# A macaron block with fp4 feed-forward layers on one Trainium2 core: the weights prepared by two ways, a new order of loads and of work, and small scale products moved between engines

## The chip, the cores and the metric

The kernel runs on one core of a Trainium2 chip. A core has five engines that work side by side, each through its own queue of instructions in the order in which they were issued: TensorE (PE in the profile, with its weight loads as PEld), VectorE (DVE), ScalarE (ACT), GpSimd (POOL), and SyncE (SP), which here issues all DMA transfers. Engines wait for one another by semaphores. Operands lie in SBUF (128 partitions), the sums of TensorE in PSUM (eight banks of 512 f32 values per partition). The metric is the time of one execution on the device in microseconds (us); lower is better.

## The reference

The input x has 4 sequences of 2048 rows of 256 values, f32. Three sublayers are added to it in turn:

```python
x = x + 0.5 * ffn(layernorm(x), w_gate, w_up, w_down)
x = x + attention(layernorm(x), Wq, Wk, Wv)      # one head, causal, scale 1/16
x = x + 0.5 * ffn(layernorm(x), w_gate, w_up, w_down)

def fp4_quant_dequant(x):                        # blocks of 16 along the last dim
    scale = maximum(max(abs(xb)) / 6, 1e-12)     # one scale a block
    idx = searchsorted(_MID, abs(xb / scale))    # nearest of 0, .5, 1, 1.5, 2, 3, 4, 6
    return _GRID[idx] * sign(xb) * scale

def fp4_linear(x, w):                            # both sides are quantized, then expanded
    return einsum('bsk,nk->bsn', fp4_quant_dequant(x), fp4_quant_dequant(w))

def ffn(x, w_gate, w_up, w_down):                # 256 -> 704 -> 256
    h = silu(fp4_linear(x, w_gate)) * fp4_linear(x, w_up)
    return fp4_linear(h, w_down)
```

Both feed-forward layers use the same three weights. The weights are f32 in memory and are quantized by the kernel itself, at its start. A quantized value is a short fp4 number times an f32 block scale, and the result has to be nearly f32-exact, so the kernel splits such a value into two f16 numbers, a high and a low part, and makes each product from three products of TensorE (high by high, high by low, low by high).

## The kernel before

**Tiles and steps.** The 8192 rows are worked on in 32 tiles of 2 x 128 rows, eight to a sequence. For a tile the stages are: load, layernorm (`layernorm`, line 629), quantization of its rows (`ffn_x`, 695), gate and up products (`ffn_gu`, 717), quantization of the hidden values (`ffn_h`, 740), down products and addition to the rows (`ffn_down`, 773), layernorm, attention (`attn_x`, `attn_vy`, `attn_scores`, `attn_exp`, `attn_pv`), and the feed-forward stages once more. The function `step(n)` (995) records one stage of each of several tiles: the scores of tile n, the first feed-forward layer of tile n + 4, the second one of tile n - 2, the load of tile n + 6. The last tile's second layer is done in two single halves of 128 rows.

**The order.** No operation is issued where the code names it. All calls go to a recorder (`Record`, 153), which notes each operation with what it depends on and a cost (`_cost`, 207). Afterwards `order` (238) plans: it runs the list of operations forwards and backwards through a model of the five engines (`_pass`, 269), with three policies of ten rounds each, and keeps the pass that ends first. A policy says how far ahead of readiness an operation may be taken and how waiting weighs against rank. The model knows of a slower TensorE after an idle window, of DMA bandwidth, and of times in which GpSimd stands while VectorE has certain operations. `rec.emit(rec.order())` (1064) then issues everything in the planned order; that is why every instruction of the profile has the same line, L339, the line of the emitting call. Which instruction is which is read from its operands' names.

**The start.** SyncE issues the loads in planned order: the first tile of x (xt), four parts of the gate and up weights (gu, of eleven blocks of 64 gate and 64 up rows three in each of the first three parts and two in the last), the down weights (dwork), the attention weights and further tiles. `prepare_gu` (510) takes for each part the block maxima (VectorE), reciprocals, divides and rounds (`cut`, 492), finds the largest scale over all parts (mx, one transpose by TensorE, one product with ones), multiplies the rounded numbers by their scaled block scales (`factors`, 502, and `times`, 486) to an f32 tile, and transposes that by f32 products with the identity matrix `ident` into PSUM, 22 blocks of 128 x 128. The high part is a ScalarE copy to f16, the low part a product that takes the high part away (`minus`, minus the identity) and a second copy. `prepare_dn` (570) does the same for the down weights, in 22 more blocks, and `prepare_attn` for the attention weights.

**The main products.** `ffn_gu` has for each of the two row halves j of a tile four groups of products, gate and up, each in two PSUM banks of 352 columns (u):

```python
T.matmul(pu[:, u, :UH], qT[:, 4 * j + 2 * a + c, :], wguT[:, b, c, c0 : c0 + UH],
```

with UH = 352; the moving operand is one run of 352 columns. A group of gate products (pg) is followed by the SiLU on ScalarE, and a group of up products (pu) by a product on VectorE that writes h. There is one buffer of two banks for each, so the next half's gate products wait for the SiLU of the last. SiLU and the softmax's exponential need different tables of ScalarE; a table load is an instruction of its own in ScalarE's queue.

**Block scales of activations.** `ffn_x` and `ffn_h` reduce a tile's blocks to their maxima (sx: xs in the profile for the rows, hs for the hidden values), take the reciprocal, round on ScalarE and VectorE (`round_e2m1`, 669), and multiply the rounded numbers with the high and the low part of the scale (`halves`, 682). The two parts are

```python
S.activation(pairs(sh), twice(sx), AF.Copy, scale=2.0**23)
V.scalar_tensor_tensor(pairs(sl), twice(sx), 2.0**23, pairs(sh), ALU.mult, ALU.subtract)
```

in `ffn_x` (xsh, xsl), and with the tile's own power of two `pt` in place of 2**23 in `ffn_h` (hsh, hsl; hmt, het and hpt are one value per partition). A DMA transpose on SyncE's queue then turns the f16 halves into xqT or hT, the operands that TensorE holds.

**Attention.** `attn_scores` copies the scores from PSUM with running maxima, and ends with nb, one value per row (the maximum times a scale, plus 15 ln 2, on VectorE), the bias of the exponential in `attn_exp`. `attn_pv` ends with rc, the reciprocal of the row's sum, times kv, a constant per partition, and the addition to xt. The names `ps` (scores), `po` (attention outputs, down products) are PSUM pools of two buffers each.

**GpSimd** has, besides constants at the start, seven operations of two columns per layernorm (`ve`, `rs` by a power, `r2` three times, `rs`, `nm`, with a letter ahead: f, a or g for the first, second and third layernorm).

Of the kernel before, what the change touches and what calls it, by code (L numbers as in the profile page):

```python
# [22 lines left out]
P = 128  # L23
# [32 lines left out]
ROUNDS = 10  # L56
POLICIES = ((100.0, 60.0), (150.0, 60.0), (200.0, 60.0))
# [95 lines left out]
class Record:  # L153


    def __init__(self):
        self.ops, self.pools = [], []
# [4 lines left out]
    def add(self, engine, real, method, args, kwargs):  # L162
# [8 lines left out]
        op.index, op.deps, op.after = len(self.ops), {}, []  # L171
# [35 lines left out]
    def _cost(self, op):  # L207
# [6 lines left out]
        if op.engine == "PE":  # L214
            t = (max(n, 64) / 2.4 + 2.2) * (4 if op.ins[0].dtype == F32 else 1)
            return t, t + 65
# [5 lines left out]
        if op.engine == "POOL":  # L222
            t = 110 if op.method == "memset" else 850 if ALU.pow in op.args else 350
            return t, t
# [13 lines left out]
    def order(self):  # L238
# [18 lines left out]
        best = None  # L257
        for policy in POLICIES:
            rank = {op: 88.0 * op.index for op in self.ops}
            for _ in range(ROUNDS):  # L260
                start, out, end = self._pass(rank, False, *policy)
                if best is None or end < best[0]:
                    best = (end, out)

                back, _, _ = self._pass({op: -start[op] - op.busy for op in self.ops}, True, *policy)
                rank = {op: -back[op] - op.busy for op in self.ops}
        return best[1]

    def _pass(self, rank, back, soon, patience):
# [3 lines left out]
        waiting = {e: [] for e in free}  # L273
# [12 lines left out]
        while len(out) < len(self.ops):  # L286
# [8 lines left out]
            t, e = best  # L295
            now = [op for op in waiting[e] if ready[op] <= t + soon]
# [24 lines left out]
            elif e == "POOL" and op.method != "memset":  # L321

                alone = 775.0 if ALU.pow in op.args else 270.0
# [3 lines left out]
            free[e] = t + op.busy + (more if e in ("PE", "POOL") else 0.0)  # L327
            end = max(end, t + op.late + more)
            for u, lag in nxt[op]:
                ready[u] = max(ready[u], t + lag + more)  # L330
# [26 lines left out]
def macaron(ctx: ExitStack, tc: tile.TileContext, x, wqT, wkT, wv, wgu, wdn, out):  # L357
# [19 lines left out]
    wguT = const.tile([P, 2, 2, 2 * DF], F16, name="wguT")  # L377
# [70 lines left out]
    GP.memset(ones, 1.0)  # L448
    minus = const.tile([P, P], F16, name="minus")
    S.activation(minus, ident, AF.Copy, scale=-1.0)  # L450

    def load_gu():
        for r, t in zip(gparts, gus):
            SY.dma_start(t, wgu[:, r, :])

    def load_rest():
        SY.dma_start(dn, wdn.rearrange("(c p) d -> p c d", p=P))
        for t, w in ((qk[:, 0], wqT), (qk[:, 1], wkT), (va[:, 0], wv)):
            SY.dma_start(t, w.rearrange("(c p) d -> p c d", p=P))

    def behind(first, op):
# [3 lines left out]
        return op  # L465

# [638 lines left out]
```

## Time and profile before

| what | value |
|---|---|
| median of three runs | 1200.46 us (1198.76, 1200.46, 1201.81) |
| the profiled execution's own time | 1200.17 us |
| its span (first to last instruction) | 1198.5 us |
| granted TensorE clock, mean | 0.999 of full speed |
| TensorE busy | 1161.6 us, 8723 matrix products |
| of it gate and up products, 352 columns, 3072 | 515.3 us |
| of it down products, 256 columns, 2176 | 264.9 us |
| VectorE, ScalarE, GpSimd busy | 1055.1, 849.4, 245.8 us |

Matrix products overlap one another in the records: a product of 352 columns has a record of 312 ns, but the starts of two neighbours are 149 ns apart. How much TensorE can do is therefore read from the distances of starts, and where it stands idle from the busy time by stages or the instructions in order of time. In such a list each row has the start, the duration, the engine, the line, the operation, output <- inputs by name (by partitions x elements and type), how many neighbours of the same kind are put together in the row, and in square brackets the idle time ahead of it and what ended that. A row of a group of instructions has, after the bar, the busy time of the group, the mean of one in ns, and the idle time before its instructions. The 40 slices of the page are 30 us long each; a digit is the busy share in tenths. The record of a busy TensorE does not show by itself that it works at its peak.

### The profile page before, as it was taken

The page shows a single profiled execution, that of the slowest core. Times are in us where ns is not written, and L with a number is a line of the kernel's source. Part 1 is how long each engine was busy: PE and PEld are TensorE (multiplying, and loading weights), DVE is VectorE, ACT ScalarE, POOL GpSimd, SP SyncE. Part 2 cuts the span into 40 slices and gives each one's busy share as a digit, 9 for nine tenths or more (in the row PEclk, how much of TensorE's full clock was granted, in tenths as well). Part 3 has the DMA queues.
Part 4 walks back from the last instruction along what each step waited for, and adds up shares of the span by engine and source line. Part 5 has one row for each costly group of instructions (what it writes and reads, how often), then busy time and mean ns, then how long its engine had stood idle before and what let it go on. Part 6 is the DMA issues. An engine that isn't in the chain of part 4 may idle for free.

```text
span 1198.5 us, 23996 instructions
## 1 busy us (share of the span) xinstructions
PE 1161.6 (97%) x8723; PEld 851.7 (71%) x8723; DVE 1055.1 (88%) x2674; ACT 849.4 (71%) x1704; POOL 245.8 (21%) x706
## 2 busy tenths in 40 slices
PE   3999999999999999999999999999999999999997
PEld 2677777777687777776777777777768777776675
DVE  7989999998779999998887999999877999978776
ACT  7768987677477987674776887677647876656552
POOL 4023321222022221121212230121202221110020
PEclk9999999999999999999999999999999999999999
DMA  6245555765464555655655556777557556646553
GB/s 213 52 76 102 97 96 114 133 122 103 81 130 92 116 101 116 125 105 103 131 95 94 110 87 111 130 133 115 101 96 113 92 92 105 105 93 105 101 111 84
DMA packets 450087, 128.27 MB, mean 107 GB/s; under 512 B 432048, under 2 KB 449200, under 8 KB 449968
## 3 DMA queue, kind: packets, MB, share of 16 engines
q1 hardware_dynamic: 449968, 126.74, 56.6%
q8 instruction: 68, 1.11, 0.4%
q14 instruction: 51, 0.42, 0.1%
HBM read 11.34 MB, written 8.39 MB: 16 GB/s over the span
## 4 chain that ended last, share of the span: by engine, by line
PE 66%; DVE 14%; ACT 13%; issue 3%; POOL 3%; DMA 1%; SPq 0%; DVEq 0%; ACTq 0%
PE po L339 28%; PE pg L339 15%; PE pu L339 14%; PE ps L339 9%; DVE h L339 4%; ACT xn L339 4%; DVE hs L339 2%; ACT sc L339 2%; ACT L339 2%; ACT h L339 1%; ACT pp L339 1%; DVE sc L339 1%; DVE xt L339 1%; DVE xs L339 1%; ACT hf L339 1%
## 5 line engine op out<-in xcount | busy, mean ns | idle before, releaser
L339 PEld LDWEIGHTS <-xqT 128*128 128x128 f16 x3072 | 299.9, 98 | 158.0 <-issue 7.5
L339 PE MATMUL po<-wdT,hT 128*128 128x256 f16 x2176 | 264.9, 274 | 5.6 <-DVE xt L339 5.2
L339 PE MATMUL pg<-wguT,xqT 128*128 128x352 f16 x1536 | 257.9, 312 | 4.9 <-ACT h L339 3.9
L339 PE MATMUL pu<-wguT,xqT 128*128 128x352 f16 x1536 | 257.4, 312 | 0.0
L339 PEld LDWEIGHTS <-hT 128*128 128x128 f16 x2176 | 213.5, 98 | 43.1 <-DMA hT<-h 4.7
L339 PE MATMUL ps<-xT,y 128*128 128x512 f16 (+2 forms) x960 | 201.2, 347 | 1.5 <-DVE sc L339 1.2
L339 PE MATMUL po<-vv,pT 128*128 128x257 f16 (+1 forms) x1632 | 194.9, 272 | 1.1 <-DMA pT<-pp 1.1
L339 PEld LDWEIGHTS <-pT 128*128 128x128 f16 x1632 | 157.8, 97 | 33.9 <-DMA pT<-pp 2.2
L339 DVE TENSOR_TENSOR h<-h,pu 128x704 f32<-128x704 f32 x128 | 112.9, 882 | 58.7 <-PE pu L339 41.1
L339 ACT ACTIVATE h<-pg,cgu 128x704 f32<-128x704 f32 x128 | 107.9, 843 | 78.9 <-PE pg L339 78.2
L339 PEld LDWEIGHTS <-y 128*128 128x128 f16 x960 | 90.6, 98 | 71.9 <-issue 3.0
L339 ACT ACTIVATE hf<-h 128x1408 f16<-128x1408 bf16 (+1 forms) x65 | 88.0, 1353 | 58.6 <-DVE h L339 58.5
L339 ACT ACT_TABLE_LOAD x90 | 115.5, 1283 | 2.3 <-PEq L1098 0.8
L339 ACT ACTIVATE sc<-sc,nb,ksc 128x128 f32<-128x128 f32 (+7 forms) x64 | 82.8, 1293 | 35.3 <-DVE nb L339 34.8
L339 DVE TENSOR_TENSOR h<-h,hinv 128x1408 f32<-128x1408 f32 (+1 forms) x65 | 103.7, 1595 | 0.5
L339 DVE TENSOR_REDUCE hs<-h 128x88 f32<-128x1408 f32 (+1 forms) x65 | 103.5, 1592 | 0.7
L339 DVE TENSOR_SCALAR_CACHE_REDUCE sc<-ps 128x512 f32<-128x512 f32 (+2 forms) x144 | 84.4, 593 | 11.2 <-PE ps L339 11.1
L339 POOL TENSOR_SCALAR gve<-gsq 128x2 f32<-128x2 f32 (+1 forms) x33 | 8.2, 249 | 415.9 <-ACT xn L339 415.9
L339 DVE TENSOR_TENSOR pp<-sc,pp 128x1024 f16<-128x1024 f32 (+4 forms) x96 | 86.4, 908 | 4.9 <-ACT pp L339 4.5
L339 POOL TENSOR_SCALAR ave<-asq 128x2 f32<-128x2 f32 x32 | 15.7, 492 | 318.4 <-ACT xn L339 213.5
L339 ACT CAST pp<-sc 128x1024 f16<-128x1024 f32 (+4 forms) x96 | 73.0, 787 | 0.4
L339 DVE SCALAR_TENSOR_TENSOR xt<-po,het,xt 128x256 f32<-128x256 f32 x128 | 60.0, 470 | 13.4 <-PE po L339 13.2
(158 smaller groups left out, 1601.0 us busy)
## 6 DMA issues: line engine op xcount, KB each, us to landing
xt<-x SPq DMA_DIRECT2D x32, 256.0 KB, 3.2
out<-xt SPq DMA_DIRECT2D x31, 256.0 KB, 2.6
pT<-pp SPq DMA_TRANSPOSE x152, 3.1
hT<-h SPq DMA_TRANSPOSE x128, 3.8
gu<-wgu SPq DMA_DIRECT2D x3, 384.0 KB, 7.4
xqT<-xn SPq DMA_TRANSPOSE x65, 3.2
xT<-xs SPq DMA_TRANSPOSE x64, 2.5
dwork<-wdn SPq DMA_DIRECT2D x1, 704.0 KB, 7.2
```

The lines of the kernel that those rows point to most:

```text
L339: op.call(*map(real, op.args), **{k: real(v) for k, v in op.kwargs.items()})
```

## The change

The diff has six parts.

- **Loads.** All loads from memory are chained in one order (`fetch`), the gate and up parts 1st, 3rd, 4th and 5th, with the first tile of x 2nd; the second tile is 6th, then the down weights and the attention weights.
- **Weights by two ways.** The first two gate/up parts are still transposed by TensorE, but with `is_transpose`, 12 blocks for the 22, and so are the 22 blocks of the down weights. The last two parts are made as f16 high and low halves directly (VectorE products with a high and a low block scale), and a DMA transpose each, on SyncE's queue, writes them to the weights' tile. The expanded scales (`factors`) go from VectorE to ScalarE.
- **Layout of the weights.** wguT goes from (high/low, k half, 1408 columns) to (11 blocks, high/low, k half, gate/up, 64). The gate and up products become 384 and 320 columns wide (six and five runs of 64 in memory) in place of 352 and 352; in PSUM the 704 results are contiguous across the border of the two banks.
- **Low parts of block scales.** hsl and xsl go from VectorE to GpSimd as plain subtractions. For that sx is scaled beforehand: in `ffn_x` by 2**23 within the operations that are there (undone in the rounding's scale), in `ffn_h` by a new ScalarE product of hs with hpt.
- **Small products of attention.** nb and the product of rc with kv go from VectorE to ScalarE.
- **The planner.** Fifteen policies of six rounds for three of ten; each pass is judged by TensorE's lost time before and after 500 us separately, and the best first half and the best second half are joined through a blended rank. A third term, `lead`, can pull the work of the start (layernorm, quantization of the first tile, and the gate/up weights) ahead. Costs of transposes, of GpSimd and of its waits are changed.

The diff, cut to its core:

```diff
--- before.py
+++ after.py
...
-ROUNDS = 10
-POLICIES = ((100.0, 60.0), (150.0, 60.0), (200.0, 60.0))
+ROUNDS = 6
+POLICIES = [(soon, 60.0, lead) for lead in (0.0, 10000.0, 20000.0) for soon in (50.0, 100.0, 150.0, 200.0, 300.0)]
+MIDDLE = 500000.0
...
-            t = 110 if op.method == "memset" else 850 if ALU.pow in op.args else 350
+            t = 110 if op.method == "memset" else 850 if ALU.pow in op.args else 330 + 2.2 * n
...
+                for h, value in enumerate(self._lost(start, end)):
+                    if best[h] is None or value < best[h][0]:
+                        best[h] = (value, policy, start, rank)
+
+                back, _, _ = self._pass({op: -start[op] - op.busy for op in self.ops}, True, policy, policy)
+                rank = {op: -back[op] - op.busy - lead[op] for op in self.ops}
+        (_, one, start, rank1), (_, two, _, rank2) = best
+
+        part = {op: min(1.0, max(0.0, (start[op] - MIDDLE) / 50000.0 + 0.5)) for op in self.ops}
+        rank = {op: rank1[op] * (1.0 - part[op]) + rank2[op] * part[op] for op in self.ops}
+        return self._pass(rank, False, one, two)[1]
...
-                alone = 775.0 if ALU.pow in op.args else 270.0
+                alone = op.busy - 80.0
...
-    wguT = const.tile([P, 2, 2, 2 * DF], F16, name="wguT")
+    wguT = const.tile([P, 11, 2, 2, 2, P // 2], F16, name="wguT")
...
+    up15 = const.tile([P, 1], F32, name="up15")
+    GP.memset(up15, 15.0 * LN2)
...
+
+    def fetch(dst, src):
+
+        loads[0] = behind(loads[0], SY.dma_start(dst, src))
+
+    def load_gu(parts):
+        for i in parts:
+            fetch(gus[i], wgu[:, gparts[i], :])
+
...
     def factors(sx, by, tw):
...
-        V.tensor_scalar(
-            tw.rearrange("p r (b i) -> p r b i", i=KI),
-            sx[:, :, :, None].to_broadcast([P, n, nb, KI]), by, 2.0**24, ALU.mult, ALU.mult,
+        S.activation(
+            tw.rearrange("p r (b i) -> p r b i", i=KI), sx[:, :, :, None].to_broadcast([P, n, nb, KI]),
+            AF.Copy, scale=by,
         )
...
     def prepare_gu():
...
+        V.tensor_scalar(cwp, cwp, 2.0**24, None, ALU.mult)
...
         for i, (r, t) in enumerate(zip(gparts, gus)):
             n = r.stop - r.start
-            factors(gsx[:, r], cwp, gtw[:, r])
-            times(t, gf16[:, r], gtw[:, r])
-            cols = slice(r.start * P // 2, r.stop * P // 2)
             if i < 2:
...
+
+                factors(gsx[:, r], cwp, gtw[:, r])
+                times(t, gf16[:, r], gtw[:, r])
+                bank = ps_gu.tile([P, 2, 512], F32, name="pu" if i else "pg")
+                for m in range(2):
+                    mm = None
                     for c in range(n):
...
                         mm = behind(mm, T.matmul(
-                            wt[:, m - ms.start, :, c, :], t[:, c, m * P : (m + 1) * P], ident, start=first, stop=last
+                            bank[:, m, c * P : (c + 1) * P], t[:, c, m * P : (m + 1) * P], ident,
+                            is_transpose=True, start=c == 0, stop=c == n - 1,
                         ))
...
+                wt = bank[:, :, : n * P].rearrange("p m (c t) -> p m c t", c=n)
+                hi, lo = (wguT[:, r, a].rearrange("p c m k j -> p m c (k j)") for a in range(2))
                 S.copy(hi, wt)
-                for m in range(ms.stop - ms.start):
+                for m in range(2):
                     T.matmul(wt[:, m], minus, hi[:, m], start=False, stop=True, skip_group_check=True)
                 S.copy(lo, wt)
+                continue
+
+            sc = gtw[:, r].bitcast(F16).rearrange("p r (a e) -> p a r e", a=2)
+            sh, sl = (sc[:, a].bitcast(dt).rearrange("p r (b i) -> p r b i", i=KI) for a, dt in ((0, BF16), (1, F16)))
+            both = gsx[:, r][:, :, :, None].to_broadcast([P, n, XB, KI])
+            S.activation(sh, both, AF.Copy, scale=cwp)
+            V.scalar_tensor_tensor(sl, both, cwp, sh, ALU.mult, ALU.subtract)
+            q = t.rearrange("p r d -> p (r d)").bitcast(F16).rearrange("p (r a d) -> p r a d", r=n, a=2)
+            for a, by in ((0, sh), (1, sl)):
+                times(q[:, :, a], gf16[:, r], by.rearrange("p r b i -> p r (b i)"))
+            SY.dma_start_transpose(
+                wguT[:, r].rearrange("p r a m k j -> p (r a m) (k j)"), q.rearrange("p r a d -> p (r a d)")
+            )
...
     def prepare_dn():
...
+        V.tensor_scalar(cw[:, MX_D : MX_D + 1], cw[:, MX_D : MX_D + 1], 2.0**24, None, ALU.mult)
...
                     mm = behind(mm, T.matmul(
                         wt[:, (c - c0) * P : (c - c0 + 1) * P], w[:, starts[c] : starts[c] + P], ident,
-                        start=c == c0, stop=c == c1 - 1,
+                        is_transpose=True, start=c == c0, stop=c == c1 - 1,
...
-        V.tensor_scalar(sx, sx, C6, CLAMP, ALU.mult, ALU.max)
+        V.tensor_scalar(sx, sx, 2.0**23 * C6, 2.0**23 * CLAMP, ALU.mult, ALU.max)
         V.reciprocal(inv, sx)
...
-        S.activation(pairs(sh), twice(sx), AF.Copy, scale=2.0**23)
-        V.scalar_tensor_tensor(pairs(sl), twice(sx), 2.0**23, pairs(sh), ALU.mult, ALU.subtract)
+        S.copy(pairs(sh), twice(sx))
+        GP.tensor_tensor(pairs(sl), twice(sx), pairs(sh), ALU.subtract)
...
-        round_e2m1(xn, inv, f)
+        round_e2m1(xn, inv, f, 2.0**23)
...
+            hj = h[:, :, j, :]
             for k in range(2):
                 pu = ps_gu.tile([P, 2, 512], F32, name="pu" if k else "pg")
...
+                for u, cs in enumerate((slice(0, 6), slice(6, 11))):
+                    w = (cs.stop - cs.start) * P // 2
+                    at = slice(512 - w, 512) if u == 0 else slice(0, w)
                     for m, (a, b) in enumerate(((0, 0), (0, 1), (1, 0))):
                         for c in range(2):
                             T.matmul(
-                                pu[:, u, :UH], qT[:, 4 * j + 2 * a + c, :], wguT[:, b, c, c0 : c0 + UH],
+                                pu[:, u, at], qT[:, 4 * j + 2 * a + c, :], wguT[:, cs, b, c, k, :],
                                 start=m == 0 and c == 0, stop=m == 2 and c == 1,
                             )
+                ph = pu.rearrange("p u n -> p (u n)")[:, P : P + DF].rearrange("p (o e) -> p o e", o=KO)
                 if k == 0:
-                    silu(S.activation(hj, by_u(pu), AF.Silu, scale=cgu[:, 0:1]))
...
-                    V.tensor_tensor(hj, hj, by_u(pu), ALU.mult)
+                    V.tensor_tensor(hj, hj, ph, ALU.mult)
...
+        S.activation(sx, sx, AF.Copy, scale=pt)
+        S.copy(pairs(sh), twice(sx))
+        GP.tensor_tensor(pairs(sl), twice(sx), pairs(sh), ALU.subtract)
...
-        V.tensor_scalar(nb, mr, ksc[:, 1:2], 15.0 * LN2, ALU.mult, ALU.add)
+        S.activation(nb, mr, AF.Identity, scale=ksc[:, 1:2], bias=up15)
...
-        V.tensor_tensor(rc, rc, kv, ALU.mult)
+        S.activation(rc, rc, AF.Copy, scale=kv)
...
-        SY.dma_start(xt[n], rows(x, n))
+        fetch(xt[n], rows(x, n))
...
+    load_gu((0,))
     load(0)
-    load_gu()
+    load_gu((1, 2, 3))
     load(1)
     load_rest()
+
+    rec.lead = 1.0
     ln_first(0)
     x1(0)
     prepare_gu()
+    rec.lead = 0.0
...
```

## The prediction

> **What bounds the kernel now.** I read the page first (busy shares, then the 40 slices), then TensorE's busy time by stages, then the instructions in order of time in the stages where TensorE is idle, and last the groups of the operations that the change moves. From the page:
>
> ```profile
> PE 1161.6 (97%) x8723; PEld 851.7 (71%) x8723; DVE 1055.1 (88%) x2674; ACT 849.4 (71%) x1704; POOL 245.8 (21%) x706
> ...
> PE   3999999999999999999999999999999999999997
> ...
> DVE  7989999998779999998887999999877999978776
> ACT  7768987677477987674776887677647876656552
> ```
>
> TensorE is the bound: 1161.6 of 1198.5 us. VectorE at 88% is the next, but no slice between the first and the last shows TensorE below 9. So an edit is worth what it takes from TensorE's own work, or from its 36.9 us of idle time. Busy time by stage (columns: the stage, its length, then PE, PEld, DVE, ACT and POOL busy, the granted clock, DMA share, GB/s) says where that idle time lies:
>
> ```profile
> 0.00:10.00 10.00, 0.00 (x0) 0.00 (x0) 3.53 (x5) 5.85 (x15) 4.25 (x22) 1.00 0.79 261
> 10.00:20.00 10.00, 0.93 (x3) 0.57 (x3) 9.96 (x28) 8.77 (x34) 3.96 (x9) 1.00 0.90 300
> 20.00:25.00 5.00, 3.69 (x17) 3.69 (x18) 4.64 (x13) 3.87 (x12) 4.43 (x8) 1.00 0.59 151
> ...
> 30.00:40.00 10.00, 8.12 (x58) 5.78 (x57) 9.55 (x30) 9.87 (x24) 0.17 (x1) 1.00 0.15 28
> ...
> 100.00:200.00 100.00, 98.97 (x738) 71.26 (x737) 97.55 (x260) 89.31 (x186) 30.11 (x84) 1.00 0.58 107
> ...
> 1180.00:1190.00 10.00, 4.80 (x30) 3.53 (x28) 8.07 (x25) 2.87 (x8) 0.00 (x0) 0.83 0.76 155
> ```
>
> 22.3 us lie in the first 40 (10.0, 9.1, 1.3 and 1.9), 9.6 after 1150, and only about 5 in the 1110 us between. In the start VectorE (9.96 of 10) and then ScalarE (9.87 of 10) are full: they prepare the weights. TensorE and ScalarE there, in order of time:
>
> ```profile
> 28.09 0.27 PE L339 MATMUL po<-ident,mx 128*1 128x128 f32 x1
> 28.20 0.33 PE L339 MATMUL pg<-wguT,minus 128*128 128x384 f16 x1
> ...
> 33.48 1.95 PE L339 MATMUL ps<-ident,dw 128*128 128x128 f32 x16
> 35.26 0.38 PE L339 MATMUL ps<-wdT,minus 128*128 128x512 f16 x1
> 37.52 1.95 PE L339 MATMUL pg<-wguT,xqT 128*128 128x352 f16 x12 [1.88 <-ACT h L339]
> ...
> 1185.90 9.25 PE L339 MATMUL po<-wdT,hT 128*128 128x256 f16 x68 [5.20 <-DVE xt L339]
> ```
>
> ```profile
> 33.19 0.30 ACT L339 COPY dw<-dw 128x64 f32<-128x64 f32 x1
> 33.32 1.15 ACT L339 ACTIVATE xn<-xt,fnm,frs 128x256 f32<-128x256 f32 x2
> 34.57 0.59 ACT L339 CAST wdT<-ps 128x512 f16<-128x512 f32 x1
> 35.05 0.26 ACT L339 ACTIVATE xsh<-xs 128x64 bf16<-128x64 f32 x1
> 35.33 1.28 ACT L339 ACT_TABLE_LOAD   x1
> 36.62 0.85 ACT L339 ACTIVATE h<-pg,cgu 128x704 f32<-128x704 f32 x1
> ```
>
> The second gate product (37.52) waits for the SiLU of the first, and that for a table load queued behind four others on ScalarE.
>
> **1. TensorE's own work.** An f32 product with the identity is two records: 16 take 35.26 - 33.48 = 1.78 us, 0.111 each, 0.22 a block. The transpose of mx, 128 f32 columns too, is one record and takes 28.20 - 28.09 = 0.11. The change turns the 22 blocks of the down weights into such transposes; they lie where TensorE is full but for the first 8. Saved: 22 x 0.11 = 2.4 us in all, 14 x 0.11 = 1.5 after the wait at 37.5. Ends: nothing (if the form counts for nothing here) and 2.4; I take the row of mx. The gate and up blocks fall from 22 to 12, their products with minus from 8 to 4; that counts only through the start of the first gate product, next.
>
> **2. The start.** SyncE now issues the four gate/up parts 1st, 3rd, 4th and 5th instead of 2nd, 4th, 8th and 11th; the last landed at 9.01 + 6.3 = 15.3 us and is now issued near 2.8, so with the median 7.4 it is there by 10.2. The second is there by 5.3 us if the 1.0 MB up to it are served in turn at the 0.33 MB a us of the first 10, by 9.2 with the median; I take 7.0. From there to the block maximum (mx, ended at 17.24) VectorE hangs on work alone: 21 instructions of 0.1 to 0.95 us, 9.5 us, to 16.5. From there to the product dw (ended 32.77) there are 42 instructions instead of 41: the 1.79 us reduction of the down weights moves in, four scale products (0.35 to 0.25 us) and two xsl (0.22) move out to ScalarE and GpSimd, and the two products of the last two parts become four of f16 with f16 (0.6 us for 768 columns, scaled from 0.88 for 1408, the pair 1.0 instead of 0.95). It ends near 31.3. On ScalarE the new order puts the table load directly behind the copy of dw; the two xn, the copy of wdT and xsh (2.0 us) come later. So copy 31.5, load 1.28, SiLU 0.85: 34.0 instead of 37.4. TensorE's first gate product starts near 27.9 (was 29.48) and all 24 have until 34, enough even if its second half waits for the two new DMA transposes, issued about 24.4 and 25.7 (3.8 us to landing as hT: 28.2 and 29.5); the next tile's xqT queues behind them on SyncE and is needed only near 38. Sum: 37.5 - 34.2 = 3.3, plus 1.5 of transposes, less 0.2 for one minus product that now comes after: 4.6 us. The low end is 1.5 (the transposes alone, if the SiLU comes no earlier). What is late next is the first hT: 12.8 us of products stand between the last up product and its use, and the old chain took 55.4 - 41.1 = 14.3; but 2.0 us of that were tile 2's row work on VectorE, which is now elsewhere. So the cover is thin, and I take 3.8 us, three quarters of the way from 1.5 to 4.6.
>
> **3. Small operations.** Off VectorE go hsl, xsl, nb and one rc:
>
> ```profile
> L339 DVE SCALAR_TENSOR_TENSOR hsl<-hs,hpt,hsh 128x176 f16<-128x176 f32 x63 | 24.8, 393 | 1.3 <-ACT hsh L339 1.1
> L339 DVE SCALAR_TENSOR_TENSOR xsl<-xs,xsh 128x64 f16<-128x64 f32 x63 | 13.6, 215 | 1.5 <-ACT xsh L339 1.5
> L339 DVE TENSOR_SCALAR nb<-mr,ksc 128x1 f32<-128x1 f32 x60 | 11.9, 201 | 0.3
> L339 DVE TENSOR_TENSOR rc<-rc,kv 128x1 f32<-128x1 f32 x64 | 9.7, 151 | 0.5
> ```
>
> That is 60 us, 1055 to 995. ScalarE gets 64 nb and 64 rc at about 0.28 (the row of het, one value with a scale from memory: 280 ns), and 65 products of hs at 0.35 (hsh of 88 columns), less 0.09 on each hsh (430 ns; by xsh's 248 for 64 columns about 340 without that scale), and four table loads fewer (86 for 90): +36 + 17 - 5 = 48, 849 to 897, 75%. No product waits for that as long as TensorE has other work: in its new order each attention output's bank is asked for again no sooner than 2.4 us of products later (old 2.8), and evacuation takes 0.8 us plus the two crossings to ScalarE. GpSimd's new products (65 of up to 176 columns, 65 of up to 64) have no row. The nearest, 2-column products, take 0.2 us undisturbed, and the longest group 0.94. I take 0.5: 65 us, POOL 311 us or 26%, no bound. The layernorms' seven steps queue behind them; ScalarE's xn waits for those. Now the rule against it. The row first: GpSimd's products fr<-frs of 2 columns average 375 ns in one layernorm and 243 in another, so something already gets in their way. The Trainium skill's "GPSIMD Engine Reference" (section 4.1) says to keep elementwise products off GpSimd, about twice as slow with two inputs, and "SBUF — State Buffer" (section "SBUF: two separate sides") that such an operation and a two-input one of VectorE shut each other out; by the 2.6 cycles an element of the former (section 3.1) the two sizes would cost an estimated 0.34 and 0.58 us with the 0.2, 60 us in all, about what VectorE is rid of. I take no gain and no loss, since VectorE isn't the bound in most stages.
>
> **4. The layout of wguT and the products 384 + 320.** Columns are the same. The moving operand is now six or five runs of 64. Two runs of 128 (po<-wdT,hT) go at 1.86 us for 17, one run of 256 at 1.31 for 12: 109.4 against 109.2 ns. At 0.2 ns a run, 4.5 more runs in 3072 products are at most 2.8 us; the other end is nothing, which I take, the difference being under the rows' rounding. SiLU and the product read 704 columns across two banks as before.
>
> **5. The new order in between** (15 policies, two halves joined). It can give back at most the 5 us idle between 40 and 1150. Its distances from products to reuse are those of before within a few tenths: median 10.25 us for attention banks in both, 29.2 and 29.0 from up products to hT. I take -1, ends -5 and +5 (the same again).
>
> **6. The end.** TensorE sits idle 5.2 us before 1185.90, and the evacuations behind it come 1.86 us apart but the first 3.7 after its start: half speed (0.83 in ten us is 1.7 us lost). The Trainium skill's "TensorE: Matmul & The Clock Gate" (Part 1) has it that an idle window of about 3.4 us halves the clock, so a gap under that would save those 1.7 us as well. Counted from the last up product of the last whole tile (two single halves follow it), VectorE's chain to that tile's second half took 10.3 us and now takes 11.0 (it holds two other up products and hsl), hT another 3.8: 14.8. Of TensorE's work 48 gate/up and 34 down products stand in front, 10.9 us: a wait of 3.9. The old start, 16.1, hung on a bank that xt freed late; xt now stands earlier. With the last halves' chains behind, the last product ends 1.7 us earlier. Ends: -1.7 and +1 (hsl on GpSimd is in the last chain twice). I take -1.
>
> **Sum.** Against the profiled execution (1200.17, span 1198.5 and 1.7 around it; 0.3 under the median of 1200.46): -3.8 - 1 - 1 = -5.8, so 1194.4.
>
> **Rivals.** (a) The start's gain is hidden: SiLU comes no earlier because the DMA transposes or the loads are late, or the first hT eats it; 1.5 stays, the end is unchanged: 1198.7. For it: ScalarE was 9.87 of 10 full there. Against: the queue in front of the table load is shorter by 2.0 us whatever happens. (b) Slower: GpSimd's products hold VectorE. In 25 us stages eleven show it busy for 23.8 to 24.8. Each loses 1.25 and gets 2.7 holds; at 0.94 us each that is 1.3 more, and what stands above 25 is some 9 us together; half of the start's gain goes too, VectorE being full there: 1200.2 + 9 - 5.8 + 1.9 = 1205. It decides from about 0.9 us a hold. Against it: the 0.94 are another operation (a power). (c) The runs of 64 do cost: from 3 ns a product, 9 us, it is slower; no row comes near.
>
> **Chances and range.** Forecast 0.55; (a) 0.24; (b) 0.10; (c) and losses in the new order (its +5) 0.11. Faster or slower means by over 0.3% (3.6 us), about what a measurement here can tell from no change: (a) is the same, (b) and (c) slower, and the edge of the forecast's own spread (1189 to 1198) falls to the same: faster 0.54, same 0.25, slower 0.21. Low end: 4.6 + 5 + 1.7 off, 1189. High end: up to just under (b), 1204.
>
> **What would show it.** First gate product near 28, the second group of gate products near 34; ident,dw in 22 records; TensorE idle 2.5 to 4 us less before 40, about 5 us in between, a gap under 4.5 near the end; DVE near 995 plus holds. Wrong if GpSimd's products pass 0.7 us, if 384 columns take over 166 ns (352 take 149), or if the idle time in between doubles.

## The result

The changed kernel takes 1208.64 us (median of four, 1207.70 to 1208.84) against 1200.88: a ratio on record of 1.0062, 95% interval 1.0050 to 1.0074. It is slower, by some 8 us, where 1194.4 was forecast. Its profiled execution took 1208.55 us with a span of 1206.8, 8.3 more than the span before. From its page, busy times and the 40 slices:

```profile
PE 1157.6 (96%) x8665; PEld 843.1 (70%) x8665; DVE 1030.6 (85%) x2417; ACT 893.0 (74%) x1892; POOL 328.9 (27%) x837
...
PE   2999999999999999999999999999999999999997
...
DVE  7988998898879999888887899889887989977676
ACT  7769997776688987776777877676758877666652
```

TensorE is busy 4.0 us less, VectorE 24.5 less, and the span still grows: TensorE's idle time went from 36.9 to 49.2 us. The slices are too coarse to show where. Busy time by stages does, first of the kernel before, then of the changed one (columns as in the prediction):

```profile
0.00:50.00 50.00, 27.74 (x189) 22.20 (x190) 41.71 (x104) 41.01 (x107) 15.89 (x50) 1.00 0.45 138
50.00:150.00 100.00, 98.53 (x747) 72.41 (x747) 93.20 (x232) 79.32 (x182) 26.37 (x76) 1.00 0.51 93
150.00:1150.00 1000.00, 996.50 (x7495) 727.54 (x7493) 885.08 (x2251) 712.93 (x1383) 199.06 (x566) 1.00 0.59 107
1150.00:1210.00 60.00, 38.87 (x299) 29.56 (x296) 35.07 (x91) 16.13 (x35) 4.49 (x14) 0.96 0.39 81
```

```profile
0.00:50.00 50.00, 25.87 (x158) 17.37 (x159) 42.72 (x96) 40.58 (x108) 20.06 (x56) 1.00 0.56 155
50.00:150.00 100.00, 93.82 (x704) 67.43 (x702) 89.42 (x213) 82.80 (x195) 33.38 (x90) 1.00 0.50 84
150.00:1150.00 1000.00, 991.14 (x7454) 723.50 (x7453) 858.58 (x2014) 745.30 (x1542) 265.51 (x664) 1.00 0.60 107
1150.00:1210.00 60.00, 46.81 (x355) 34.84 (x353) 39.88 (x96) 24.36 (x49) 9.96 (x27) 0.96 0.47 92
```

TensorE's idle time is what its busy time falls short of the length of the stage; the last stage ends with the span, at 48.5 and 56.8 us after 1150:

| stage, us | before | changed | difference |
|---|---|---|---|
| 0 to 50 | 22.26 | 24.13 | +1.9 |
| 50 to 150 | 1.47 | 6.18 | +4.7 |
| 150 to 1150 | 3.50 | 8.86 | +5.4 |
| 1150 to the end | 9.63 | 9.99 | +0.4 |
| busy time | 1161.6 | 1157.6 | -4.0 |

The sum is +8.4. The idle time of the first stage does not mean a late start, since the same stage holds fewer instructions. TensorE and ScalarE there, in order of time:

```profile
27.90 0.48 PE L357 MATMUL pg<-wguT,xqT 128*128 128x384 f16 x2 [0.21 <-ACT wguT L357]
...
34.66 1.95 PE L357 MATMUL pg<-wguT,xqT 128*128 128x384 f16 x12 [1.34 <-ACT h L357]
...
43.73 1.95 PE L357 MATMUL pg<-wguT,xqT 128*128 128x384 f16 x12
45.52 1.95 PE L357 MATMUL pu<-wguT,xqT 128*128 128x384 f16 x12
...
51.42 2.03 PE L357 MATMUL po<-wdT,hT 128*128 128x256 f16 x17
```

```profile
32.20 0.24 ACT L357 COPY dw<-dw 128x64 f32<-128x64 f32 x1
32.47 1.28 ACT L357 ACT_TABLE_LOAD   x1
33.76 0.85 ACT L357 ACTIVATE h<-pg,cgu 128x704 f32<-128x704 f32 x1
```

The table load stands directly behind the copy of dw, the second group of gate products starts at 34.66 (before 37.52), and the first product with hT at 51.42 (before 55.42). So at 51 us the kernel is 4.0 us ahead, and it loses 12.3 from there on. Of these 12.3 only some 10.5 are idle time. Up to the first product with hT TensorE is busy 33.0 us before and 27.2 in the changed kernel; from there on it has the same work but for one product, and is busy 1.8 us longer with it (1130.4 us for 1128.6). So busy time holds lost time too, and the 4.0 of the table understate what TensorE was spared. What TensorE waited for, by the waits of the whole span (total, times, longest), first before and then changed:

```profile
...
PE po L339 <- DVE xt L339: 5.2, 1, 5.2
PE pg L339 <- ACT h L339: 3.9, 8, 1.9
...
PE po L339 <- DMA pT<-pp: 1.1, 2, 0.8
```

```profile
...
PE po L357 <- DMA hT<-h: 6.4, 5, 3.4
PE pg L357 <- ACT h L357: 5.8, 8, 1.6
PE po L357 <- DMA pT<-pp: 3.8, 5, 1.1
...
PE pg L357 <- DMA xqT<-xn: 1.2, 2, 0.8
```

Before, no wait for hT is in this list. Now TensorE waits five times for hT and five times for pT, operands that a DMA transpose brings. The longest of these, 3.4 us for hT at the end, stands where the kernel before waited 5.2 us for xt. The loss is in between. From 50 to 1150 alone the list is, before and changed:

```profile
PE pg L339 <- ACT h L339: 2.0, 7, 0.5
...
PE po L339 <- DMA pT<-pp: 0.3, 1, 0.3
```

```profile
PE pg L357 <- ACT h L357: 3.2, 6, 1.6
PE po L357 <- DMA hT<-h: 2.9, 4, 1.2
PE po L357 <- DMA pT<-pp: 2.8, 4, 1.1
...
```

Of 15.0 us idle there (before 5.0), hT and pT make 5.7, the SiLU's result h 3.2, and the rest is spread over waits of under 1 us each. The question for the runs was what makes so many operands late.

### The profile page after: what moved, and what is told of

Read it like the earlier page. It is cut to its first block, busy times and chain, and to the rows that moved or that the text cites. A ratio compares the mean times of both kernels' runs of the same rounds, so it can differ in the third digit from the quotient of the medians.

```text
span 1206.8 us, 24015 instructions
## 1 busy us (share of the span) xinstructions
PE 1157.6 (96%) x8665; PEld 843.1 (70%) x8665; DVE 1030.6 (85%) x2417; ACT 893.0 (74%) x1892; POOL 328.9 (27%) x837
## 4 chain that ended last, share of the span: by engine, by line
PE 50%; DVE 20%; ACT 17%; DMA 5%; issue 4%; POOL 3%; SPq 0%; DVEq 0%; POOLq 0%; ACTq 0%
PE po L357 21%; PE pg L357 11%; PE pu L357 10%; PE ps L357 8%; DVE h L357 7%; ACT xn L357 4%; DVE hs L357 3%; ACT L357 2%; DMA hT<-h 2%; ACT h L357 2%; ACT hf L357 2%; DVE xt L357 2%; ACT sc L357 2%; DVE pp L357 1%; DVE sc L357 1%
## 5 line engine op out<-in xcount | busy, mean ns | idle before, releaser
L357 PE MATMUL po<-wdT,hT 128*128 128x256 f16 x2176 | 261.5, 274 | 7.3 <-DMA hT<-h 6.4
L357 PE MATMUL pg<-wguT,xqT 128*128 128x384 f16 (+1 forms) x1536 | 258.3, 312 | 7.6 <-ACT h L357 5.8
L357 PE MATMUL pu<-wguT,xqT 128*128 128x384 f16 (+1 forms) x1536 | 255.0, 312 | 0.0
L357 POOL TENSOR_TENSOR hsl<-hs,hsh 128x176 f16<-128x176 f32 (+1 forms) x65 | 51.9, 799 | 283.6 <-ACT hsh L357 240.1
L357 DVE TENSOR_TENSOR pp<-sc,pp 128x1024 f16<-128x1024 f32 (+4 forms) x96 | 86.8, 913 | 11.8 <-ACT pp L357 11.2
L357 DVE TENSOR_SCALAR_CACHE_REDUCE sc<-ps 128x512 f32<-128x512 f32 (+2 forms) x144 | 84.3, 592 | 10.1 <-PE ps L357 9.8
L357 POOL TENSOR_TENSOR xsl<-xs,xsh 128x64 f16<-128x64 f32 (+1 forms) x65 | 31.5, 485 | 196.2 <-ACT xsh L357 192.2
```

The lines of the kernel that those rows point to most:

```text
L357: op.call(*map(real, op.args), **{k: real(v) for k, v in op.kwargs.items()})
```

## The experiments

All times are medians; ratios are those on record, to the kernel before, run on the same chip. The five groups of runs were spread over four chips, on which the kernel before took 1201.1 to 1201.8 us, so a comparison across groups is good to about 1 us at best. The cuts of code are shortened.

**First, which part.** Three theories for the 12 us: GpSimd's low parts, the new choice of the order, or a start whose gain can't be kept.

e1, the start and the layout alone:

```diff
- GP.tensor_tensor(pairs(sl), twice(sx), pairs(sh), ALU.subtract)      # both places
+ V.scalar_tensor_tensor(...)                                          # as before
- S.activation(nb, ...); S.activation(rc, rc, AF.Copy, scale=kv)
+ V.tensor_scalar(nb, ...); V.tensor_tensor(rc, rc, kv, ALU.mult)
- fifteen policies, two halves, new costs of GpSimd
+ three policies, ten rounds, the best whole pass, old costs of GpSimd
```

> The changed kernel with its loads, weights and layout of wguT, but hsl, xsl, nb and rc made where they were before, and the order planned as before (three policies, the best whole pass, the old costs of GpSimd). The trace of the changed kernel shows the first 50 us gained 4.0 us and what comes after lost 12.4. If the loss comes from GpSimd's products or from the new choice of the order, this kernel keeps the 4.0: about 1197 us, 0.4% under before. If the start's gain is given back by itself, because the first hidden values can't be made faster, it is 1200 to 1201.

Measured 1205.55, ratio 1.0034 (1.0022 to 1.0047). Neither: slower than before, without GpSimd's products and without the joined order. Its idle time is 27.3 us up to 50 and 5.9 from 50 to 150, then only 2.3 up to 1150: here the start itself came out worse, with the same loads and weights in another order.

e2, hsl and xsl in their old form (shown for hsl):

```diff
- S.activation(sx, sx, AF.Copy, scale=pt)
- S.copy(pairs(sh), twice(sx))
- GP.tensor_tensor(pairs(sl), twice(sx), pairs(sh), ALU.subtract)
+ S.activation(pairs(sh), twice(sx), AF.Copy, scale=pt)
+ V.scalar_tensor_tensor(pairs(sl), twice(sx), pt, pairs(sh), ALU.mult, ALU.subtract)
```

> The changed kernel with hsl and xsl back on VectorE in their old form, planned anew in the new way. If GpSimd's products are the cause (hsl takes 0.80 us there, 0.39 on VectorE), most of the 12.4 us is back: 1197 to 1200. If the new choice of the order is the cause, 1206 to 1209.

Measured 1198.18, ratio 0.9974 (0.9964 to 0.9985): 10.5 under the changed kernel.

e3, the changed kernel's order with another engine at the same places:

```diff
+ GV = rec.engine("POOL", nc.vector)           # planned as GpSimd's, issued to VectorE
- GP.tensor_tensor(pairs(sl), twice(sx), pairs(sh), ALU.subtract)      # both places
+ GV.tensor_tensor(pairs(sl), twice(sx), pairs(sh), ALU.subtract)
```

> The changed kernel in exactly its own order, only that the subtractions of hsl and xsl are issued to VectorE at the places where they stood for GpSimd (the order is not planned anew). VectorE gets 65 x about 0.35 + 65 x about 0.2 = 36 us more. If GpSimd's durations and holds are the cause: 1198 to 1201. If the order is: 1207 to 1210.

Measured 1209.29, ratio 1.0066 (1.0053 to 1.0078): no difference to the changed kernel. In the traces TensorE and ScalarE have the same sequence of instructions in both, and so have VectorE and GpSimd but for the low parts. Taken alone, e2 speaks for GpSimd and e3 against it.

e4, the old choice of the order with all operations changed:

```diff
- POLICIES = [(soon, 60.0, lead) for lead in (0.0, 10000.0, 20000.0) for soon in (50.0, ..., 300.0)]
+ POLICIES = ((100.0, 60.0, 0.0), (150.0, 60.0, 0.0), (200.0, 60.0, 0.0))   # and the best whole pass
```

> The changed kernel with only the choice of the order put back: three policies of ten rounds, the best whole pass in place of two joined halves, no lead; the costs stay new. If the joined order is the cause of the loss: 1197 to 1201. If GpSimd's products are: 1206 to 1209.

Measured 1212.46, ratio 1.0087 (1.0073 to 1.0101). The new choice by itself is not what costs; the order that the old one makes is 4 us worse.

**Second, GpSimd or ScalarE's product beside it; nb and rc; the planner alone.** e5 keeps the new form and the new choice, and only names another engine, so that the plan is made for it:

```diff
- GP.tensor_tensor(pairs(sl), twice(sx), pairs(sh), ALU.subtract)      # both places
+ V.tensor_tensor(pairs(sl), twice(sx), pairs(sh), ALU.subtract)
```

> The changed kernel, planned anew, with the two subtractions recorded and issued on VectorE, everything else of the new form kept (the ScalarE product of hs with hpt too). With hsl and xsl back in their old form the kernel came to 1198.2 us; two things were undone there, GpSimd's part and that product. If GpSimd is the cause: 1197 to 1200 again. If the longer chain over ScalarE is: 1206 to 1209.

Measured 1191.83, ratio 0.9921 (0.9908 to 0.9934): 16.8 under the changed kernel, faster than the kernel before and than either theory had it. e6 has the low parts as in e2 and the choice as in e4:

> hsl and xsl in their old form on VectorE, and the order chosen in the old way (the best whole pass of three policies): the fourth cell beside the changed kernel (1208.6), low parts on VectorE (1198.2) and old choice (1212.5). If what costs is that the low parts are on GpSimd, whichever order is chosen: 1199 to 1202, some 10 under 1212.5. If 1198.2 was one lucky order: 1205 or more.

Measured 1201.31, ratio 1.0003 (0.9994 to 1.0011), 11.2 under e4. e7 is e2 with nb and rc on VectorE:

```diff
- S.activation(nb, mr, AF.Identity, scale=ksc[:, 1:2], bias=up15)
+ V.tensor_scalar(nb, mr, ksc[:, 1:2], 15.0 * LN2, ALU.mult, ALU.add)
- S.activation(rc, rc, AF.Copy, scale=kv)
+ V.tensor_tensor(rc, rc, kv, ALU.mult)
```

> The low parts as well as nb and rc back on VectorE, planned in the new way: what is left of the change is the start, the layout of the gate and up weights and the planner. If nb and rc on ScalarE cost nothing and bring nothing: 1197 to 1200. If they spare VectorE on the path: 1200 to 1203. If ScalarE's extra turns cost: 1194 to 1197.

Measured 1204.48, ratio 1.0029 (1.0017 to 1.0040), 6.3 over e2. e8 is the kernel before with the planner's choice alone:

```diff
- POLICIES = ((100.0, 60.0), (150.0, 60.0), (200.0, 60.0))      # ten rounds, best whole pass
+ POLICIES = [(soon, 60.0, lead) for lead in ...]                 # fifteen, six rounds, joined halves, lead
```

> The kernel before with only the new choice of the order (fifteen policies, two joined halves, lead), its costs unchanged. If the new choice is good by itself: 1195 to 1199. If it makes no difference: 1200 to 1202. If joined orders have less cover: 1204 or more.

Measured 1201.12, ratio 1.0001 (0.9992 to 1.0009). Up to here, but for e3, it looked settled: the low parts on GpSimd, 10 to 17 us.

**Third, one by one, and with a longer cost.** e9 takes e5's edit for xsl only and e10 for hsl only, so that the other one stays on GpSimd; e11 plans both 0.5 us longer; e12 joins e5's halves elsewhere:

```diff
- t = 110 if op.method == "memset" else 850 if ALU.pow in op.args else 330 + 2.2 * n
+ t = 110 if op.method == "memset" else 850 if ALU.pow in op.args else 330 + 2.2 * n + 500 * (n > 2)   # e11
- MIDDLE = 500000.0
+ MIDDLE = 400000.0                                                                                    # e12, on e5
```

> The changed kernel with only hsl on GpSimd, xsl on VectorE, planned anew. With both on GpSimd the time is 1208.6, with both on VectorE 1191.8. If the loss lies in the chain to hT (hsl waits for VectorE's products and the down products wait for hT): 1203 to 1209. If it lies with the layernorm's steps that queue behind many GpSimd products, both share it: about 1200.

> The changed kernel with only xsl on GpSimd, hsl on VectorE, planned anew. If the loss lies in the chain to hT: 1191 to 1195, since xsl takes 0.49 us and its rows are quantized well ahead. If both share it: about 1200.

> The changed kernel with one number of the planner changed: hsl and xsl are planned with 0.5 us more on GpSimd (about 1.22 and 0.97, near the longest in the trace, 1.25 and 1.35). If the loss comes from waits that the plan didn't foresee: 1196 to 1202. If the chain over GpSimd is simply too long, planned or not: 1206 to 1210.

> The fastest kernel so far (both subtractions on VectorE, 1191.8) with the halves joined at 400 us in place of 500, which means nothing but another order of the same instructions. It shows how much of a difference the order alone makes. If 1191.8 stands for these operations: 1190 to 1195. If it was a lucky order: 1197 to 1202, as with the old form (1198.2 and 1201.3).

Measured: e9 1205.50 (ratio 1.0034, 1.0022 to 1.0046), e10 1203.08 (1.0013, 1.0004 to 1.0022), e11 1202.31 (1.0004, 0.9995 to 1.0013), e12 1190.47 (0.9907, 0.9893 to 0.9921). xsl alone seems to cost nearly what hsl alone does (11.3 and 13.7 over e5, together more than both at once, 16.8), which does not fit the theory of the chain to hT. e11, 6.3 under the changed kernel, lies at the edge of what unforeseen waits would give; but a third of TensorE's instructions stand elsewhere in it, so it is another order too. e12 proved no test: in its order only 0.3% of TensorE's instructions stand more than five places from where they stand in e5.

**Fourth, the missing cell, and nb and rc twice more.** e13 is e5's order with the two subtractions issued to GpSimd at the same places:

```diff
+ VG = rec.engine("DVE", nc.gpsimd)            # planned as VectorE's, issued to GpSimd
- V.tensor_tensor(pairs(sl), twice(sx), pairs(sh), ALU.subtract)       # both places
+ VG.tensor_tensor(pairs(sl), twice(sx), pairs(sh), ALU.subtract)
```

> Exactly the order of the kernel with both subtractions on VectorE (1191.8), only that they are issued to GpSimd at the same places. It is the fourth cell of planned for / issued to: GpSimd, GpSimd 1208.6; GpSimd, VectorE 1209.3; VectorE, VectorE 1191.8. If GpSimd's own durations and VectorE's holds cost the time: 1200 to 1210. If what costs is the order that a plan for GpSimd makes: 1190 to 1194.

Measured 1195.89, ratio 0.9959 (0.9947 to 0.9971). It lies between the two forecasts. Of the 16.8 us only 4.1 are GpSimd's own in this order (the intervals of e5 and e13 are apart), and in the changed kernel's order they were -0.7 (e3), which is within the noise:

| planned for | issued to GpSimd | issued to VectorE |
|---|---|---|
| GpSimd | 1208.6 | 1209.3 (e3) |
| VectorE | 1195.9 (e13) | 1191.8 (e5) |

The rows differ by 12.7 and 17.5, the columns by 4.1 and -0.7. Between these two plans the order decides far more than the engine. e14 is e5 with e7's edit of nb and rc, e15 is e8 with that edit the other way round:

> Both subtractions on VectorE (1191.8), and nb and rc put back there too, planned anew. If nb and rc on ScalarE are worth about 6 us, as the pair 1204.5 and 1198.2 says: 1197 to 1199. If that pair was luck of the order: 1190 to 1194.

> The kernel before with the new choice of the order (1201.1) and only nb and rc on ScalarE. If they are worth 6 us by themselves: 1194 to 1197. If not: 1199 to 1203.

Measured: e14 1204.69 (ratio 1.0031, 1.0016 to 1.0045), 12.9 over e5; e15 1209.34 (1.0076, 1.0063 to 1.0090), 8.2 over e8. So nb and rc on ScalarE come out 12.9 better in one pair and 8.2 worse in another. Both are outside what was expected. Each pair also compares two orders, so neither figure can be put down to nb and rc.

**Fifth, other orders of the same instructions.** Only the weight of waiting in the choice is changed, from 60 to 50 (e16 on the changed kernel, e17 on e5) and 70 (e18 on e5); 25 to 33% of TensorE's instructions move by more than five places:

```diff
- POLICIES = [(soon, 60.0, lead) for lead in ...
+ POLICIES = [(soon, 50.0, lead) for lead in ...
```

> The changed kernel, instructions unchanged, in another order: the weight of waiting in the planner's choice is 50 in place of 60; a third of TensorE's instructions move by more than five places. If GpSimd's part sets the time: 1205 to 1213, as in its two other orders (1208.6, 1212.5). If 1208.6 is mostly this one order: anything from 1194 up.

> The kernel with both subtractions on VectorE (1191.8) in another order, weight of waiting 50. If VectorE's form sets the time: 1190 to 1197. If 1191.8 is a lucky order: 1198 to 1206.

> As the one before, weight of waiting 70: a third order. Same expectations: 1190 to 1197, or 1198 to 1206.

Measured: e16 1199.48 (ratio 0.9990, 0.9982 to 0.9999), e17 1201.59 (1.0004, 0.9996 to 1.0013), e18 1198.36 (0.9979, 0.9970 to 0.9988). The changed kernel itself, with no instruction changed, is 9.2 us faster in another order, and a little under the kernel before; the fast kernel is 6.5 and 9.8 us slower in two other orders. At weight 50 the kernel with GpSimd's products is even 2.1 under the one without.

The waits of TensorE in e5, for comparison with those above:

```profile
...
PE po L357 <- DMA hT<-h: 4.0, 2, 3.8
...
PE pg L357 <- ACT h L357: 1.6, 3, 0.8
PE pg L357 <- DMA xqT<-xn: 1.3, 3, 0.5
```

And its busy time by stages:

```profile
50.00:150.00 100.00, 97.38 (x739) 71.75 (x737) 92.75 (x232) 82.19 (x199) 26.84 (x77) 1.00 0.50 89
150.00:1150.00 1000.00, 998.95 (x7549) 732.99 (x7547) 875.73 (x2139) 750.90 (x1548) 200.09 (x566) 1.00 0.60 109
1150.00:1210.00 60.00, 30.60 (x225) 22.15 (x223) 28.80 (x75) 15.45 (x35) 5.09 (x14) 0.96 0.31 59
```

A good order leaves TensorE idle for 2.6 us from 50 to 150 and 1.1 in the next 1000; its only long wait for hT is the one at the end. The changed kernel loses 6.2 and 8.9 in these stages, in waits of at most 1.6 us each. And the same 8665 matrix products are busy 1152.7 us in e5's order and 1157.6 in the changed kernel's, both at a mean granted clock of 0.999: of the 17.9 us between the two spans 13.0 are idle time and 4.9 busy time.

**What stands.** Shown: the changed kernel's own instructions can take 1199.5 as well as 1208.6 us, so its 8 us are not a fixed cost of its parts but come with the order in which they were issued. e4 and e11 are such orders as well, with 1212.5 and 1202.3. Shown for two fixed orders: the low parts on GpSimd cost 4.1 and -0.7 us. Not settled: whether plans with GpSimd's products come out worse on the mean. With all changed operations the four orders gave 1208.6, 1212.5, 1202.3 and 1199.5 (mean 1205.7); with the subtractions on VectorE three gave 1191.8, 1201.6 and 1198.4 (mean 1197.3; e12, nearly the order of the first, is left out). The groups overlap. TensorE's idle time from 50 to 1150 leans the same way: in the four orders, as named, it is 15.0, 13.9, 9.8 and 12.3 us (e16's profiled execution took 1203.1 us, 3.6 over its median), in the three 3.7, 9.2 and 7.4, and before 5.0. Equally unsettled is the worth of nb and rc on ScalarE, and what in an order makes it a good one: the planner's `_cost` reckons the transpose of hT with 3.34 us (2250 + 908 x 1.2 ns) where the median is 3.9, and the waits for it in the changed kernel would fit that, but no run changed this number. e12, 1190.47 us, is the fastest, 0.93% under the kernel before.

## Why the prediction was wrong

**Step 5, the new order in between, is the one that failed.** It said that the order "can give back at most the 5 us idle between 40 and 1150", found the distances from products to reuse "those of before within a few tenths", and took -1 with ends of -5 and +5. Between 50 and 1150 the idle time grew by 10.1 us, twice the upper end. The lower end came from a row, the 5 us that were there to be had. The upper one, "the same again", came from none: nothing in the profile bounds how much a new order can lose. And the distances counted in products say how much cover there is, not how long the thing covered takes: 5.7 of the 15.0 us idle from 50 to 1150 are waits for hT and pT to land, where the kernel before had 0.3. That the order loses it, and not the instructions, is shown by other orders: idle from 50 to 1150 are 9.8 us in e11 and 12.3 in e16, with the very same instructions, and 5.5 in e13, with GpSimd's products in e5's order. Which feature of an order decides stays open. The prediction named the sign for it under "Wrong if": "the idle time in between doubles". From 40 to 1150 it went from 5.0 to 15.0.

**Step 2, the start, was right, and was then lost.** Forecast and then measured, in us: first gate product 27.9 and 27.90; table load behind the copy of dw, 31.5 and 32.47; second group 34.2 and 34.66; first product with hT earlier by the "3.8 us" taken and by 4.0. The sign it named for this, 2.5 to 4 us less idle time before 40, was the wrong one: idle time there grew by 1.9, and the gain came out of 5.8 us less busy time. The cover of the first hT, which it called thin, was enough: the row at 51.42 has no wait ahead of it. What went was 4.7 us from 50 to 150, where four waits for later hT make 2.9. That this is no law of the start is seen in e5, which has the same loads and weights and is idle there for only 1.1 us more than the kernel before. So rival (a) did not happen as worded: the SiLU came earlier, and it was not "the first hT" that ate the gain.

**Step 1** holds: the dw blocks now take one record each (eight in 0.95 us, 40.09 to 41.04), 0.12 a block in place of 0.22.

**Step 4** holds: twelve gate products of 384 and 320 columns go at 1.79 us (45.52 - 43.73), as the twelve of 352 did (39.31 - 37.52). The six runs of 64 cost nothing that can be seen, and rival (c) falls.

**Step 3** had the durations about right. The moved operations after the change:

```profile
L357 POOL TENSOR_TENSOR hsl<-hs,hsh 128x176 f16<-128x176 f32 x63 | 50.6, 803 | 276.7 <-ACT hsh L357 238.1 <-DVE h L357 21.5 <-DVE hf L357 16.5
L357 POOL TENSOR_TENSOR xsl<-xs,xsh 128x64 f16<-128x64 f32 x63 | 30.7, 488 | 190.1 <-ACT xsh L357 186.0 <-DVE xs L357 3.8
L357 ACT ACTIVATE nb<-mr,up,ksc 128x1 f32<-128x1 f32 x60 | 22.7, 379 | 38.3 <-DVE mr L357 38.3
L357 ACT ACTIVATE hs<-hs,hpt 128x88 f32<-128x88 f32 x63 | 22.6, 359 | 0.2
```

hsl and xsl were taken at 0.5 us and are 0.80 and 0.49, so hsl passed the 0.7 that was named as a sign; nb was taken at 0.28 and is 0.38; hs at 0.35 is 0.36. POOL came to 328.9 for 311 and ScalarE to 893 for 897. VectorE's busy time fell by 24.5 us where 60 were counted: these small instructions start 82 ns (the median before) ahead of the end of the one before them, so a row is longer than what taking it away saves (258 instructions, by estimate some 20 us); longer products on VectorE add 5, and the rest was not traced. e3 points the same way: there, in the same order, 35 us of such rows more make VectorE busy only 13.0 us longer, while its larger products are some 5 us shorter. "No gain and no loss" for the products on GpSimd was off by 4.1 us in one order and right in the other. The rule of the Trainium skill ("GPSIMD Engine Reference", section 4.1) that speaks against such products is borne out by the rows: the same subtraction for hsl takes 330 ns on VectorE in e5, 520 undisturbed on GpSimd and 803 there on the mean, 1.6 and 2.4 times. The estimate of 0.58 us for hsl, worked out from the page, is near the 0.52 us of an undisturbed one and short of the mean.

**Rival (b)** ended on the right side and near the size (1205), by a mechanism that the runs reject. VectorE is hardly held: of its larger products h<-hf,hsh went from 885 to 931 ns, xn<-xn,xinv from 686 to 704, xs<-xn,xs from 682 to 709. That is 2.9 + 1.1 + 0.9 = 4.9 us in all, not 0.94 us a hold, and in e3, where GpSimd has none of it, the time is the same; in e5's order the products on GpSimd cost 4.1 us (e13).

**Step 6, the end:** -1 was taken, +0.4 came. The wait in front of the last 68 products was forecast at 3.9 us and is 3.41:

```profile
1183.04 1.96 PE L357 MATMUL pg<-wguT,xqT 128*128 128x384 f16 x12 [0.83 <-DMA xqT<-xn]
...
1193.91 9.57 PE L357 MATMUL po<-wdT,hT 128*128 128x256 f16 x68 [3.41 <-DMA hT<-h]
```

But three waits of 0.83 to 1.26 us stand ahead of it, and the granted clock is 0.83 from 1190 to 1200, as it was from 1180 to 1190 before, with a gap of 5.20; so the shorter gap saved nothing of the slow clock.

The chances followed from this. Five terms, two of them put at nothing, were added to one figure, and the order, whose loss no row bounded, had the largest spread: over the 20 kernels here the medians run from 1190.5 to 1212.5, and orders of the very same instructions lie up to 13.0 us apart (1199.5 and 1212.5).

## What to carry to other kernels

Where a planner places every instruction, any edit can draw a new order of everything, and the draw can be worth more than the edit; its spread has to be measured with a few orders of the same instructions before a difference is put down to the edit. To tell an engine's own cost from that of the plan, keep the order and issue the operation to the other engine at its place, both ways; the pair with a new plan alone (1208.6 and 1191.8) said 16.8 us where the fixed orders said 4.1 and -0.7. A term of a forecast that no row bounds upward needs a range of its own, not the mirror image of its gain.

## What the runs showed of the hardware

GpSimd waits for VectorE, and that is most of what its low parts take over their own time (hsl 0.80 us on the mean, 0.52 undisturbed). Half of the 63 rows of hsl take at most 0.52 us; the 16 that began during a product h<-hf,hsh of VectorE take 1.19 on the mean, and make 10.7 of the 17.9 us that all 63 took over 0.52. A low part alone, one that starts just after a VectorE product of two SBUF operands, and one that starts just ahead of such a product, from the changed kernel's GpSimd and VectorE in order of time:

```profile
189.07 0.52 POOL L357 TENSOR_TENSOR hsl<-hs,hsh 128x176 f16<-128x176 f32 x1 [1.69 <-ACT hsh L357]
```

```profile
909.53 1.23 POOL L357 TENSOR_TENSOR hsl<-hs,hsh 128x176 f16<-128x176 f32 x1 [10.75 <-ACT hsh L357]
```

```profile
909.49 0.89 DVE L357 TENSOR_TENSOR h<-hf,hsh 128x1408 f16<-128x1408 f16 x1 [1.75 <-ACT hsh L357]
```

```profile
247.01 0.52 POOL L357 TENSOR_TENSOR hsl<-hs,hsh 128x176 f16<-128x176 f32 x1 [8.30 <-DVE hf L357]
```

```profile
247.12 1.17 DVE L357 TENSOR_TENSOR h<-hf,hsh 128x1408 f16<-128x1408 f16 x1
```

The first takes 0.52 us. The second starts 0.04 us after VectorE's product and ends 0.38 us after it: it waits for that product to end. The product itself keeps its usual 0.89 us. The third starts 0.11 us ahead of VectorE's product and keeps its 0.52 us; now the product is the one that takes longer, 1.17 us. The Trainium skill ("SBUF — State Buffer", section "SBUF: two separate sides") says that of two such instructions the one that starts first has the shared port to itself and the other waits for all of it; these rows agree with that.
